# Pairwise products on two engines: fewer waits in VectorE's order, a larger VectorE share, one more cut in the first piece

## The chip, the cores and the metric

The kernel runs on one core of a Trainium2 chip. The metric is the device time of one execution in microseconds (us). Times before are of 14 executions; the profile is of one.

## The reference

The input is a matrix of 4096 rows and 256 columns in fp32. For each row, the output holds the product of every pair of its elements, upper triangle only, row by row of that triangle: 256 products with element 0, 255 with element 1, and so on, 32,896 in all.

```python
d = inputs.shape[1]
dot = jnp.einsum('bi,bj->bij', inputs, inputs)
iu, ju = jnp.triu_indices(d)
return dot[:, iu, ju]
```

The output has 539 MB and the input 4 MB.

## The kernel before

A partition holds 32 rows of the input, which are all loaded at the start (three loads, L246). The work goes by groups of two rows a partition (REPEAT = 2), 16 groups. The 32,896 columns of a group are cut into three pieces of 10,944, 10,976 and 10,976 columns (`even_borders`, L26). So there are 48 pieces; I call the three pieces of one group a row of pieces. A piece is computed into one of two places in on-chip memory (`places`, L123) and stored from there with one DMA of some 11 MB (L226). Of the first piece of all, four parts are stored on their own, cut at the columns in FIRST (L23), so that the stores can start early.

A piece consists of runs (`runs`, L31): the stretch of products of one element i with all j from i on. `split` (L71) gives the first runs of a piece to ScalarE and the rest to VectorE: it moves runs to ScalarE until VectorE's estimated time (`vector_time`, L67: 68 ns an operation and 1.046 ns an element) is within a budget of so many ns a column (BUDGETS, L22) or ScalarE would be the later one. ScalarE takes one activation for each run and group row (L206), with element i as its scale. VectorE takes one tensor_tensor for a run or for two runs together, both group rows at once (L185). An operation for two runs computes one junk element behind its second run, which the next operation of the same stretch overwrites. So the order on VectorE matters: `interleave` (L57) cuts VectorE's runs in two halves and takes operations from both in turn, and each operation waits until the operation two places before it has finished (`Work.add` with `back` 1, L144) and counts itself on the semaphore `v_own`.

Each engine runs its own loop over passes of six pieces (`all_pieces`, L230). Two pieces are made ahead of the loop. For each piece VectorE takes the place's semaphore `free` (L178; `take` at L134 waits and subtracts in one instruction), raises `go` for ScalarE (L179), computes, waits for its own last operation and raises `v_done` (L193). ScalarE takes `go` (L202), computes, waits for its last one and raises `a_done` (L215). SyncE takes both (L223, L224) and issues the store; the 16 DMA engines that carry it raise `free` by one each when their part has landed. At the start of a group VectorE and ScalarE copy its input rows into tiles of their own (L175, L199). The first piece's parts are counted on `head`, which GpSimd turns into `free` (L252).

Of the kernel before, what the change touches and what calls it, by code (L numbers as in the profile page):

```python
# [9 lines left out]
AF = mybir.ActivationFunctionType  # L10
ALU = mybir.AluOpType
# [3 lines left out]
REPEAT = 2  # L15
PIECES = 3
PLACES = 2
PASS = 6
AHEAD = 2


BUDGETS = [0.95, 0.8, 0.85]  # L22
FIRST = [512, 1536, 3584]  # L23


def even_borders(lo: int, hi: int, pieces: int) -> list[int]:  # L26
# [30 lines left out]
def interleave(block: list) -> list:  # L57


    half = len(block)  # L60
    while half and len(vector_ops(block[:half])) > len(vector_ops(block[half:])):
        half -= 1
    a, b = vector_ops(block[:half]), vector_ops(block[half:])
    return [op for k in range(max(len(a), len(b))) for ops in (a, b) for op in ops[k : k + 1]]


def vector_time(block: list) -> float:  # L67
# [15 lines left out]
def window(ap: bass.AP, free: list) -> bass.AP:  # L83
    return bass.AP(ap.tensor, ap.offset, [list(ap.ap[0]), *free])


@with_exitstack
def kernel(
    ctx: ExitStack, tc: tile.TileContext, x: bass.AP, out: bass.AP
):  # L90

    nc = tc.nc
    n, d = x.shape
    width = out.shape[1]
    each, groups = REPEAT * d, n // (P * REPEAT)
    rounds = PASS // PIECES
    passes = groups // rounds
    assert n % (P * REPEAT) == 0 and width == d * (d + 1) // 2 and width % UNIT == 0
    assert PASS % PLACES == 0 and AHEAD == PLACES and PASS % PIECES == groups % rounds == 0  # L110
    borders = even_borders(0, width, PIECES)
    spans = list(zip(borders, borders[1:]))
    slot = max(b - a for a, b in spans)

    x_in = x.rearrange("(p g) d -> p (g d)", p=P)
    x_out = out.rearrange("(p h q r) c -> h q p r c", p=P, q=rounds, r=REPEAT)

    pool = ctx.enter_context(tc.tile_pool(name="all", bufs=1))
    xt = pool.tile([P, passes, rounds * each], F32, name="x")

    xv = pool.tile([P, each + 1], F32, name="xv")
    xa = pool.tile([P, each], F32, name="xa")
    places = [pool.tile([P, REPEAT, slot], F32, name=f"o{k}") for k in range(PLACES)]  # L123
    ctx.enter_context(tc.tile_critical())  # L124

    def semaphore(name: str):
        return ctx.enter_context(nc.semaphore(name))

    free = [semaphore(f"free{k}") for k in range(PLACES)]
    head, v_done, a_done, go = (semaphore(s) for s in ("head", "v_done", "a_done", "go"))  # L130
    loads = [0, each, groups // 2 * each, groups * each]
    loaded = [semaphore(f"loaded{k}") for k in range(len(loads) - 1)]

    def take(engine, sem, value: int):  # L134
        engine.wait_ge(sem, value).then_inc(sem, -value)  # L135

    class Work:

        def __init__(self, engine, name: str):
            self.engine, self.sem, self.count, self.marked = engine, semaphore(name), 0, 0

        def add(self, ins, back: int, mark: bool = True):  # L144
            if self.count > back:
                ins._wait_ge(self.sem, self.count - back)
            if mark:
                ins.then_inc(self.sem, 1)
                self.count += 1

        def end(self):
            return self.engine.wait_ge(self.sem, self.count)

        def restart(self):
            self.engine.sem_inc(self.sem, -self.count)  # L155
            self.count = 0

    v, a = Work(nc.vector, "v_own"), Work(nc.scalar, "a_own")

    def x_of(h, q: int) -> bass.AP:  # L160
        return xt[:, bass.ds(h, 1), q * each : (q + 1) * each].rearrange("p o d -> p (o d)")

    def blocks(p: int, ahead: bool):

        lo, hi = spans[p % PIECES]
        cuts = [lo, *(FIRST if ahead and p == 0 else []), hi]
        for a, b in zip(cuts, cuts[1:]):
            block = runs(d, a, b)
            k = split(block, 0.0 if ahead else BUDGETS[p % PIECES] * REPEAT * (b - a))
            yield a - lo, b - lo, block[:k], block[k:], lo  # L170

    def vector(h, pieces: range, ahead: bool):
        for p in pieces:
            if p % PIECES == 0:
                v.add(nc.vector.tensor_copy(xv[:, :each], x_of(h, p // PIECES)), 0)  # L175
                v.end()
            if not ahead:
                take(nc.vector, free[p % PLACES], 16)  # L178
                nc.vector.sem_inc(go, 1)  # L179
            for _, _, _, block, lo in blocks(p, ahead):  # L180
                for (i, j, at, length), m in interleave(block):
                    at -= lo

                    v.add(
                        nc.vector.tensor_tensor(  # L185
                            places[p % PLACES][:, :, at : at + m * length],
                            window(xv[:, j:], [[d, REPEAT], [1, m], [1, length]]),
                            window(xv[:, i:], [[d, REPEAT], [1, m], [0, length]]),
                            ALU.mult,
                        ),  # L190
                        1,
                    )
                v.end().then_inc(v_done, 1)  # L193
        v.restart()

    def scalar(h, pieces: range, ahead: bool):
        for p in pieces:
            if p % PIECES == 0:
                a.add(nc.scalar.activation(xa, x_of(h, p // PIECES), AF.Copy), 0)  # L199
                a.end()  # L200
            if not ahead:
                take(nc.scalar, go, 1)  # L202
            for _, _, block, _, lo in blocks(p, ahead):
                todo = [(run, r) for run in block for r in range(REPEAT)]
                for (i, j, at, length), r in todo:
                    ins = nc.scalar.activation(  # L206
                        places[p % PLACES][:, r, at - lo : at - lo + length],
                        xa[:, r * d + j : r * d + j + length],
                        AF.Copy,
                        scale=xa[:, r * d + i : r * d + i + 1],  # L210
                    )
                if todo:
                    ins.then_inc(a.sem, 1)
                    a.count += 1
                a.end().then_inc(a_done, 1)  # L215
        a.restart()

    def sync(h, pieces: range, ahead: bool):
        for p in pieces:
            place = places[p % PLACES]  # L220
            parts = list(blocks(p, ahead))
            for lo, hi, *_, base in parts:
                take(nc.sync, v_done, 1)  # L223
                take(nc.sync, a_done, 1)  # L224
                to = x_out[bass.ds(h, 1), p // PIECES, :, :, base + lo : base + hi]
                nc.sync.dma_start(to.rearrange("o p r c -> p (o r) c"), place[:, :, lo:hi]).then_inc(  # L226
                    free[p % PLACES] if len(parts) == 1 else head, 16
                )

    def all_pieces(engine, pieces_of):  # L230
        pieces_of(0, range(AHEAD), True)
        if engine is not nc.sync:
            for sem in loaded[1:]:
                engine.wait_ge(sem, 16)
        kind = engine.engine
        with nc.Fori(
            0,
            passes,
            engines=OrderedEngineSet([kind]),
            head_slot={kind: 0} if engine is not nc.sync else {},  # L240
        ) as h:
            pieces_of(h, range(AHEAD, PASS), False)
            with engine.If(h < passes - 1):
                pieces_of(nc.s_assert_within(h + 1, 0, passes - 1), range(AHEAD), False)

    for (lo, hi), sem in zip(zip(loads, loads[1:]), loaded):  # L246
        nc.sync.dma_start(xt.rearrange("p h d -> p (h d)")[:, lo:hi], x_in[:, lo:hi]).then_inc(sem, 16)
    nc.vector.memset(xv[:, each:], 0.0)  # L248
    for engine in (nc.vector, nc.scalar):
        engine.wait_ge(loaded[0], 16)  # L250

    take(nc.gpsimd, head, 16 * (len(FIRST) + 1))  # L252
    nc.gpsimd.sem_inc(free[0], 16)
    for engine, pieces_of in ((nc.vector, vector), (nc.scalar, scalar), (nc.sync, sync)):
        all_pieces(engine, pieces_of)
    for k in range(PLACES):
        take(nc.sync, free[k], 16)
    for sem in loaded:
        take(nc.sync, sem, 16)

# [26 lines left out]
```

## Time and profile before

| | |
|---|---|
| median of 14 executions | 1273.59 us (1273.39 to 1273.87) |
| the profiled execution | 1273.57 us |
| its span in the profile | 1271.5 us |
| VectorE (DVE) busy | 915.4 us, 1712 instructions |
| ScalarE (ACT) busy | 606.4 us, 1837 instructions |
| DMA, mean over the span | 427 GB/s |
| a store of a whole piece, issue to landing | 33.1 us median |

The span runs from the first to the last instruction that the profile shows; 2.1 us of the execution's time lie around it. "DVEq", "ACTq" and "SPq" are the engines' sequencers, which wait, branch and issue. L135 is the body of the helper `take`, so a wait there is one for `free`, `go`, `v_done` or `a_done`, by engine. In the table by stage, the columns are: the stretch, its length, busy time and number of instructions of VectorE, ScalarE and GpSimd, the granted TensorE clock, the mean busy share of the 16 DMA engines, and what they moved in GB/s. A packet is put there in the stretch where it falls for the most part, so in stretches of one or two packets the share can go above one.

### The profile page before, as it was taken

Reading aid. Unit: us, or ns where it says so; the run is one execution under the profiler, and the core shown is the slowest. Engines: PE = TensorE matmul, PEld = TensorE weight load, DVE = VectorE, ACT = ScalarE, POOL = GpSimd, SP = SyncE. Lnnn points to the kernel's source line nnn. Section 1 sums busy time; section 2 is a strip of 40 time slices with the busy share of each in tenths; the row PEclk is TensorE's granted clock in tenths of the full one; section 3 lists DMA queues with packets and bytes.
Section 4 is the critical chain, followed back from the end, with each engine's and each line's share of the span. In section 5 each row is a group of like instructions: output and inputs, shape, how many; then the busy total and the mean of one; then the engine's idle time right before and its main releaser. Section 6 shows DMA issues by size and latency. Waiting matters only on the chain. (4 is left out here: it accounts for less than half of the span.)

```text
span 1271.5 us, 4308 instructions
## 1 busy us (share of the span) xinstructions
DVE 915.4 (72%) x1712; ACT 606.4 (48%) x1837; POOL 0.2 (0%) x4
## 2 busy tenths in 40 slices
DVE  8767786777768776687757877578776787677860
ACT  8625535354363533635337352473524635156350
POOL 0000000000000000000000000000000000000000
DMA  9999999999999999999999999999999999999998
GB/s 380 436 438 424 438 423 439 424 438 435 426 439 424 437 424 438 428 433 437 425 419 442 419 442 420 440 421 419 442 420 441 420 441 420 420 441 424 437 420 356
DMA packets 14310, 543.21 MB, mean 427 GB/s; under 512 B 864, under 2 KB 864, under 8 KB 1504
## 3 DMA queue, kind: packets, MB, share of 16 engines
q1 hardware_dynamic: 14304, 543.17, 99.3%
q14 instruction: 6, 0.05, 0.0%
HBM read 4.19 MB, written 538.97 MB: 427 GB/s over the span
## 5 line engine op out<-in xcount | busy, mean ns | idle before, releaser
L185 DVE TENSOR_TENSOR o<-xv 128x736 f32<-128x736 f32 (+61 forms) x1695 | 908.5, 616 | 311.6 <-DVEq L135 311.0
L206 ACT ACTIVATE o<-xa 128x198 f32<-128x198 f32 (+44 forms) x1820 | 595.1, 419 | 621.1 <-ACTq L135 620.6
L175 DVE COPY xv<-x 128x512 f32 (+1 forms) x16 | 6.8, 427 | 8.9 <-DVEq L155 4.2
L199 ACT ACTIVATE xa<-x 128x512 f32 (+1 forms) x16 | 10.1, 629 | 5.1 <-ACTq L155 3.4
L199 ACT ACT_TABLE_LOAD x1 | 1.3, 1283 | 3.9 <-DMA x<-in_r_inputs_dram 3.9
L248 DVE MEMSET xv<- 128x1 f32 x1 | 0.1, 59 | 1.0 <-SPq L124 1.0
L274 POOL MEMSET const-uint8-127<- 128x1 uint8 x1 | 0.1, 102 | 0.0
L274 POOL MEMSET const-bfloat16-1.0<- 128x1 bf16 x1 | 0.1, 101 | 0.0
L274 POOL MEMSET const-float32-0.0<- 128x1 f32 x1 | 0.1, 98 | 0.2 <-issue 0.2
L274 POOL MEMSET const-float32-1.0<- 128x1 f32 x1 | 0.1, 98 | 0.0
## 6 DMA issues: line engine op xcount, KB each, us to landing
out_dram<-o SPq DMA_DIRECT2D x32, 10976.0 KB, 33.1
out_dram<-o SPq DMA_DIRECT2D x15, 10944.0 KB, 30.7
out_dram<-o SPq DMA_DIRECT2D x1, 7360.0 KB, 20.0
x<-in_r_inputs_dram SPq DMA_DIRECT2D x1, 2048.0 KB, 13.1
out_dram<-o SPq DMA_DIRECT2D x1, 2048.0 KB, 12.6
x<-in_r_inputs_dram SPq DMA_DIRECT2D x1, 1792.0 KB, 7.3
out_dram<-o SPq DMA_DIRECT2D x1, 1024.0 KB, 11.0
out_dram<-o SPq DMA_DIRECT2D x1, 512.0 KB, 10.4
```

Of the source, the lines that this page charges most:

```text
L175: v.add(nc.vector.tensor_copy(xv[:, :each], x_of(h, p // PIECES)), 0)
L185: nc.vector.tensor_tensor(places[p % PLACES][:, :, at : at + m * length], window(xv[:, j:], [[d, REPEAT], [1, m], [1, length]]), window(xv ...
L199: a.add(nc.scalar.activation(xa, x_of(h, p // PIECES), AF.Copy), 0)
L206: ins = nc.scalar.activation(places[p % PLACES][:, r, at - lo : at - lo + length], xa[:, r * d + j : r * d + j + length], AF.Copy, scale=x ...
L248: nc.vector.memset(xv[:, each:], 0.0)
L274: nc = _bacc.Bacc("TRN2", target_bir_lowering=False, num_devices=1)
```

## The change

- BUDGETS goes from 0.95, 0.8, 0.85 to 1.0, 1.0, 0.95 ns a column and group row, so VectorE gets more runs of each piece and ScalarE fewer.
- FIRST gets a fourth cut at 6400: the first piece is stored in five parts.
- `interleave` cuts VectorE's runs in SETS stretches (2 in this version) with equal numbers of operations, and tells for each operation which earlier one of its stretch it has to follow: only one that comes behind an operation for two runs has such a predecessor.
- An operation waits only where it has such a predecessor that no earlier wait covers (for the predecessor or the operation two places before it, whichever is later), and only operations that are waited for count on `v_own`, besides the last of a piece where a wait for it follows.
- The place's `free` is no longer lowered at each piece: VectorE waits for 16, then 32, then takes 48, in the three uses of a place in a pass. Where it waits, that wait raises `go`; where it takes, an uncounted operation raises `go`. ScalarE's first activation waits for `go` itself, against a running count.
- At most pieces the last operation raises `v_done` or `a_done` itself; only at the last piece of a group (and of a range of pieces, on VectorE) does the engine still wait for its own last operation and then raise it.

```diff
+SETS = 2
-BUDGETS = [0.95, 0.8, 0.85]
-FIRST = [512, 1536, 3584]
+BUDGETS = [1.0, 1.0, 0.95]
+FIRST = [512, 1536, 3584, 6400]
...
 def interleave(block: list) -> list:
-    half = len(block)
-    while half and len(vector_ops(block[:half])) > len(vector_ops(block[half:])):
-        half -= 1
-    a, b = vector_ops(block[:half]), vector_ops(block[half:])
-    return [op for k in range(max(len(a), len(b))) for ops in (a, b) for op in ops[k : k + 1]]
+    sets, k = [], 0
+    for left in range(SETS, 0, -1):
+        share = -(-len(vector_ops(block[k:])) // left)
+        end = k
+        while end < len(block) and len(vector_ops(block[k : end + 1])) <= share:
+            end += 1
+        if left == 1:
+            end = len(block)
+        sets.append(vector_ops(block[k:end]))
+        k = end
+    order, last = [], {}
+    for step in range(max(map(len, sets))):
+        for s, ops in enumerate(sets):
+            if step < len(ops):
+                order.append((*ops[step], last.get(s)))
+                last[s] = len(order) - 1 if ops[step][1] == 2 else None
+    return order
...
     def vector(h, pieces: range, ahead: bool, done: int = 0) -> int:
...
             if not ahead:
-                take(nc.vector, free[p % PLACES], 16)
-                nc.vector.sem_inc(go, 1)
+                if use(p) < uses:
+                    nc.vector.wait_ge(free[p % PLACES], 16 * use(p)).then_inc(go, 1)
+                else:
+                    take(nc.vector, free[p % PLACES], 16 * uses)
             for _, _, _, block, lo in blocks(p, ahead):
-                for (i, j, at, length), m in interleave(block):
+                order = interleave(block)
+                own = (p + 1) % PIECES == 0 or p == pieces[-1]
+                counted, waits = {len(order) - 1} if own else set(), {}
+                for k, (*_, before) in enumerate(order):
+                    if before is not None and before > max(waits.values(), default=-1):
+                        waits[k] = max(before, k - 2)
+                        counted.add(waits[k])
+                lets_go = -1
+                if not ahead and use(p) == uses:
+                    lets_go = next(k for k in range(len(order)) if k not in counted)
+                number = {k: done + 1 + c for c, k in enumerate(sorted(counted))}
+                for k, ((i, j, at, length), m, _) in enumerate(order):
...
+                    if k in waits:
+                        ins._wait_ge(v_own, number[waits[k]])
+                    if k in counted:
+                        ins.then_inc(v_own, 1)
+                    if k == lets_go:
+                        ins.then_inc(go, 1)
+                done += len(counted)
-                v.end().then_inc(v_done, 1)
-        v.restart()
+                if own:
+                    nc.vector.wait_ge(v_own, done).then_inc(v_done, 1)
+                else:
+                    ins.then_inc(v_done, 1)
+        return done

     def scalar(h, pieces: range, ahead: bool):
...
-            if not ahead:
-                take(nc.scalar, go, 1)
...
+                if not ahead:
+                    turns += 1
+                    todo[0]._wait_ge(go, turns)
+                if not todo:
+                    nc.scalar.sem_inc(a_done, 1)
+                elif (p + 1) % PIECES:
+                    todo[-1].then_inc(a_done, 1)
+                else:
+                    todo[-1].then_inc(a_own, 1)
+                    done += 1
+                    nc.scalar.wait_ge(a_own, done).then_inc(a_done, 1)
...
     for k in range(PLACES):
-        take(nc.sync, free[k], 16)
+        take(nc.sync, free[k], 16 * uses)
```

More of the change, by code (lines that the diff above doesn't have):

```diff
@@ L135, in take @@
         engine.wait_ge(sem, value).then_inc(sem, -value)
[L137 to L158, printed above, removed]
+    v_own, a_own = semaphore("v_own"), semaphore("a_own")
     def x_of(h, q: int) -> bass.AP:
@@ L170, in blocks, with use, vector @@
             yield a - lo, b - lo, block[:k], block[k:], lo
-    def vector(h, pieces: range, ahead: bool):
+    uses = PASS // PLACES
+    def use(p: int) -> int:
+        return (p - AHEAD) % PASS // PLACES + 1
+    def vector(h, pieces: range, ahead: bool, done: int = 0) -> int:
         for p in pieces:
+            place = places[p % PLACES]
             if p % PIECES == 0:
-                v.add(nc.vector.tensor_copy(xv[:, :each], x_of(h, p // PIECES)), 0)
-                v.end()
+                ins = nc.vector.tensor_copy(xv[:, :each], x_of(h, p // PIECES))
+                if done:
+                    ins._wait_ge(v_own, done)
+                ins.then_inc(v_own, 1)
+                done += 1
+                nc.vector.wait_ge(v_own, done)
@@ L177, in vector @@
             if not ahead:
-                take(nc.vector, free[p % PLACES], 16)
-                nc.vector.sem_inc(go, 1)
+                if use(p) < uses:
+                    nc.vector.wait_ge(free[p % PLACES], 16 * use(p)).then_inc(go, 1)
+                else:
+                    take(nc.vector, free[p % PLACES], 16 * uses)
             for _, _, _, block, lo in blocks(p, ahead):
-                for (i, j, at, length), m in interleave(block):
-                    at -= lo
[L184 to L191, printed above, removed]
-                    )
@@ new lines, in vector @@
+                if not ahead and use(p) == uses:
+                    lets_go = next(k for k in range(len(order)) if k not in counted)
+                number = {k: done + 1 + c for c, k in enumerate(sorted(counted))}
+                for k, ((i, j, at, length), m, _) in enumerate(order):
+                    at -= lo
+                    ins = nc.vector.tensor_tensor(
+                        place[:, :, at : at + m * length],
+                        window(xv[:, j:], [[d, REPEAT], [1, m], [1, length]]),
+                        window(xv[:, i:], [[d, REPEAT], [1, m], [0, length]]),
+                        ALU.mult,
+                    )
+                    if k in waits:
+                        ins._wait_ge(v_own, number[waits[k]])
+                    if k in counted:
+                        ins.then_inc(v_own, 1)
+                    if k == lets_go:
+                        ins.then_inc(go, 1)
@@ L196, in scalar @@
+                done += len(counted)
[4 more added lines that the diff above has]
+        return done
     def scalar(h, pieces: range, ahead: bool):
+        done = turns = 0
         for p in pieces:
+            place = places[p % PLACES]
             if p % PIECES == 0:
-                a.add(nc.scalar.activation(xa, x_of(h, p // PIECES), AF.Copy), 0)
-                a.end()
@@ L201, in scalar @@
-            if not ahead:
-                take(nc.scalar, go, 1)
+                nc.scalar.activation(xa, x_of(h, p // PIECES), AF.Copy).then_inc(a_own, 1)
+                done += 1
+                nc.scalar.wait_ge(a_own, done)
             for _, _, block, _, lo in blocks(p, ahead):
[L204 to L207, printed above, removed]
+                todo = [
+                    nc.scalar.activation(
+                        place[:, r, at - lo : at - lo + length],
@@ L211, in scalar @@
                     )
[L212 to L216, printed above, removed]
+                    for i, j, at, length in block
+                    for r in range(REPEAT)
+                ]
+                if not ahead:
[7 more added lines that the diff above has]
+                    todo[-1].then_inc(a_own, 1)
+                    done += 1
+                    nc.scalar.wait_ge(a_own, done).then_inc(a_done, 1)
+        for sem, count in ((a_own, done), (go, turns)):
+            if count:
+                nc.scalar.sem_inc(sem, -count)
     def sync(h, pieces: range, ahead: bool):
@@ L230, in all_pieces @@
     def all_pieces(engine, pieces_of):
-        pieces_of(0, range(AHEAD), True)
+        done = pieces_of(0, range(AHEAD), True)
+        if engine is nc.vector:
+            nc.vector.sem_inc(v_own, -done)
         if engine is not nc.sync:
@@ L241, in all_pieces @@
         ) as h:
-            pieces_of(h, range(AHEAD, PASS), False)
+            done = pieces_of(h, range(AHEAD, PASS), False)
             with engine.If(h < passes - 1):
-                pieces_of(nc.s_assert_within(h + 1, 0, passes - 1), range(AHEAD), False)
+                nxt = nc.s_assert_within(h + 1, 0, passes - 1)
+                if engine is nc.vector:
+                    nc.vector.sem_inc(v_own, -vector(nxt, range(AHEAD), False, done))
+                else:
+                    pieces_of(nxt, range(AHEAD), False)
+        if engine is nc.vector:
+            nc.vector.sem_inc(v_own, -done)
     for (lo, hi), sem in zip(zip(loads, loads[1:]), loaded):
```

## The prediction, made before the changed kernel ran

> **What bounds the kernel now.** I began with the page's slices and its table of DMA queues:
>
> ```profile
> DMA  9999999999999999999999999999999999999998
> GB/s 380 436 438 424 438 423 439 424 438 435 426 439 424 437 424 438 428 433 437 425 419 442 419 442 420 440 421 419 442 420 441 420 441 420 420 441 424 437 420 356
> ...
> q1 hardware_dynamic: 14304, 543.17, 99.3%
> ```
>
> The 16 DMA engines are busy in every slice but the last, and the one queue fills 99.3% of their time with 543 MB. The stores set the end; the two compute engines only refill places between them. Next I took the waits and the groups, to see which engine waits for whom:
>
> ```profile
> L185 DVE TENSOR_TENSOR o<-xv 128x736 f32<-128x736 f32 (+61 forms) x1695 | 908.5, 616 | 311.6 <-DVEq L135 311.0
> L206 ACT ACTIVATE o<-xa 128x198 f32<-128x198 f32 (+44 forms) x1820 | 595.1, 419 | 621.1 <-ACTq L135 620.6
> ```
>
> VectorE (L185) stands idle for 311 us and ScalarE (L206) for 621 us, nearly all of it behind L135, the helper that takes a place's "free" or the "go". Compute is early, everywhere. Then the timeline of the last row of three pieces:
>
> ```profile
> 1165.94 20.75 DVE L185 TENSOR_TENSOR o<-xv 128x996 f32<-128x996 f32 x22 [6.82 <-DVEq L135]
> 1165.99 5.66 ACT L206 ACTIVATE o<-xa 128x256 f32<-128x256 f32 x14 [7.18 <-ACTq L135]
> 1187.06 50.57 SPq L226 DMA_DIRECT2D out_dram<-o  x3
> 1191.99 17.52 DVE L185 TENSOR_TENSOR o<-xv 128x768 f32<-128x768 f32 x24 [5.30 <-DVEq L135]
> 1192.02 12.49 ACT L206 ACTIVATE o<-xa 128x7 f32<-128x7 f32 x36 [20.37 <-ACTq L135]
> 1218.01 18.88 DVE L185 TENSOR_TENSOR o<-xv 128x468 f32<-128x468 f32 x60 [8.50 <-DVEq L135]
> 1218.04 18.39 ACT L206 ACTIVATE o<-xa 128x98 f32<-128x98 f32 x62 [13.52 <-ACTq L135]
> ```
>
> A fill takes 20.75, 17.52 or 18.88 us, and fills start 26 us apart, one store's length. Last, the table by stage, laid over the end of the last store:
>
> ```profile
> 1264.00:1266.00 2.00, 0.00 (x0) 0.00 (x0) 0.00 (x0) 1.00 0.82 351
> 1266.20:1267.80 1.60, 0.00 (x0) 0.00 (x0) 0.00 (x0) 1.00 0.06 27
> 1267.80:1269.40 1.60, 0.00 (x0) 0.00 (x0) 0.00 (x0) 1.00 0.06 27
> ```
>
> After 1266.1 us a DMA share of 0.06 is left, one engine in sixteen at 27 GB/s, until 1269.6 us. So one DMA engine, which I call the straggler, ends 3.6 us behind the other fifteen. The landing records of each store (sixteen increments) say how it came to that. The store that lands around 1187.86 has fifteen increments between 1187.77 and 1187.96 and the last at 1191.76; its lag is 1.8 us at the first whole piece, about 2 us at 300 us, and 3.4 to 4.0 us from 600 us on. The packets show the fifteen standing still for about 0.46 us, from 1187.5 to 1187.96, before the store issued at 1187.06 begins, while the straggler still works on the previous one. **The straggler is the bound**: it has no gap after 2 us, and the end is its work, not the fifteen engines' and not the fills.
>
> **What the Trainium skill says.** "DMA: Bandwidth & Descriptors", section "Specifications", gives the fabric's ceiling as 435 GB/s; the table by stage has 432, 432 and 431 GB/s over the three stores before 1217.4, so nothing is to be had from more overlap. The same page, "Why a DMA increments its semaphore by 16 and not by 1", says that only the full 16 means that all has landed; here a fill starts 0.26 us after the sixteenth increment (1165.68 to 1165.94), thus behind the straggler. The same page, "Latency and other measured facts", says that two of the sixteen engines are usually slower and calls its cause a guess; this trace has one, unnumbered. "VectorE: DVE Perf Modes", section "The DRAIN you can't avoid", reports that a semaphore after each of eight copies costs nothing over one after the last. The trace agrees as far as it goes: the 22 operations of the 20.75 us fill hold 18,384 elements a partition, and with 68 ns each (the planner's own figure) that leaves 1.047 ns an element, with no room for a stall by waits.
>
> **The change, part by part.**
>
> *Waits and counts.* The text has four stretches and every third, but SETS is 2, and the loop over `order` still finds nearly every operation two places behind its predecessor in the same stretch. Counting by the code: 104 to 108 counted operations in a row of three pieces against 106 before. So this edit is about nothing. The `free` and `go` traffic loses one or two sequencer steps a piece (0.02 us for L179 in the chain), on a path with slack: 0.
>
> *Larger share.* By the planner's budgets, elements and operations of VectorE go from 18,384/22 to 19,388/22 in the first piece of a row, 15,148/24 to 19,108/29 in the second, 13,922/60 to 15,622/63 in the third. At 1.047 ns and 68 ns: 21.8 us, 22.0 us, and 20.6 + 0.2 (what the third misses now, 18.88 against 18.66) = 20.9 us. ScalarE falls from 14, 36 and 62 operations to 10, 16 and 48, some 4, 5.5 and 15 us, always done before VectorE. The longest fill grows from 20.75 to 22.0 us. Does that reach the straggler? From its landing to the next store's first packet: 0.26 (start) + fill + 0.37 (1186.69 to 1187.06) + 0.9 (issue to first packet) = fill + 1.53. It has its other store to do meanwhile, and needs the new one 1191.41 - 1165.68 = 25.7 us after the landing (1191.41 is its landing at 1191.76 less the 0.35 us that lie between a last packet and its increment). So a fill may last 24.2 us; 22.0 leaves 2.2 us. What is late next is the fifteen: at the present lag they stand still whenever a fill exceeds 20.75 - 0.46 = 20.3 us, so now also in the second piece, by up to 1.7 us, until the lag settles lower, near 2.5 us. That costs nothing at the end. Cover gone means a fill over 24.2 us: then each excess counts once a piece.
>
> *What the straggler pays for the compute.* Its store takes 26.35 us beside the third piece's fill, 26.08 beside the first's, 26.01 (a smaller one) beside the second's, and 25.95 for the very last, with no compute beside it (25.88 for the smaller size, by bytes). The excess is 0.40, 0.13 and 0.14 us, 0.67 a row, about 10 us in all the 15.3 rows. The fifteen show none of it. It follows the number of instructions: 122, 36 and 60 products beside them, thus 3.3, 3.6 and 2.3 ns each; by VectorE's alone (60, 22, 24) 6.7, 5.9 and 5.8 ns. No view separates the two, so I bound it. If every instruction counts, sequencer steps too, a row goes from 252 to about 217: -14% of 0.67 is -0.09 us a row, -1.4 us. If only VectorE's count, 106 to 114 products give +8 x 6 ns = +0.05 a row, +0.7 us. If instructions and semaphore counts weigh alike (374 to 341), -9%, -0.9 us. I take this middle one.
>
> *One more border in the first piece.* It splits the 7360 KB store at 6400. The DMA engines are full from 2 us on anyway (the 4 MB input fills the hole), so an earlier store gains 0. It adds 16 packets to each engine: the measured packets (14336 B in 535 ns, 29440 B in 1091 ns) make a split one dearer by some 9 ns, x16 = +0.15 us. Bounds -0.1 to +0.3.
>
> *Sum.* The profiled execution took 1273.57 us (the median is 1273.59): 2.0 until the first packet, 1267.6 of the straggler, 1.9 to the end of the span at 1271.5, and 2.1 around it. 1273.57 - 0.9 + 0.15 = **1272.8 us**. Both bounds give 1272.2 to 1274.4 with the border's cost; another page of instructions fetched (309 ns a packet early in the trace) adds 0.3 either way.
>
> **Rivals.** *ScalarE's instructions are what slows the straggler.* For it: its packets beside ScalarE's work are longer than those beside VectorE alone (1635 against 1630 ns in the first piece's fill). Against it: by ScalarE's counts the excess is 6.5, 9.3 and 3.9 ns, a worse fit. 112 to 74 takes a third, 0.23 us a row, 3.5 us: 1270.2 us. *Nothing that matters changes*, or VectorE's operations alone matter: counts stay, the bound stays, 1273.8 to 1274.4, say 1274.1 us. *Slower: the fill becomes the bound.* If the k - 2 waits held VectorE after all, by 60 ns an operation, the third piece would take 20.9 + 3.8 = 24.7 us, over the 24.2 by 0.5, less the 0.2 that the next store gives back: 15 times 0.3 us, 1278 us. It decides from 24.2 us on. Against it: the same waits stand in the kernel before, and the idle time on VectorE is all behind L135.
>
> **How the numbers follow.** A measurement of this kernel tells about 0.2% from no change, 2.5 us: the border lies at 1271.0 and 1276.1. Likeliest, as summed, 0.56 (1271.6 to 1273.6); VectorE alone or nothing, 0.25; ScalarE's relief, 0.14, nearly all of it beyond 0.2%; fill-bound, 0.05. So faster 0.13, same 0.82, slower 0.05. The range takes in the first two and the better half of the relief: 1270.5 to 1274.6.
>
> **What would show it.** Fills of about 21.8, 22.0 and 20.9 us on VectorE and still 16 DMA engines in lockstep; a tail of one engine of about 2.5 instead of 3.6 us; rows of 78.35 us instead of 78.45 between the straggler's landings. It is wrong if rows are shorter than 78.25 (ScalarE's relief) or a fill exceeds 24 us and the straggler shows a gap before a store. A change in the first 70 us of more than 0.5 us would mean that I misread the border.

## The result and the profile after

The changed kernel takes 1291.13 us (1290.98 to 1291.20) against 1273.58 us: the ratio is 1.0138, with a 95% interval of 1.0128 to 1.0148. It is 17.5 us slower, where 1272.8 us was forecast. The kernel before was timed again beside each experiment, at a median of 1273.49 to 1273.64 us; ratios and differences below are to that time.

The page of the changed kernel, its slices and its DMA queue:

```profile
DMA  9999999999999999999999999899998999999999
GB/s 381 444 421 430 436 393 414 436 434 416 413 414 436 434 428 401 414 436 435 435 393 414 436 435 435 371 436 435 435 435 386 421 435 436 414 413 414 435 436 392
...
q1 hardware_dynamic: 14576, 543.17, 98.0%
```

The bytes of the stores are the same, but the engines' share has fallen from 99.3 to 98.0%, and slices of 371 to 414 GB/s stand between slices at 435. The stores now have holes. The groups of the page tell that VectorE isn't what fills the time (columns: busy time and mean of one; then the idle time before them and what ended most of it):

```profile
L202 DVE TENSOR_TENSOR o<-xv 128x124 f32<-128x124 f32 (+61 forms) x1818 | 1023.2, 643 | 217.1 <-DMA out_dram<-o 148.0
L231 ACT ACTIVATE o<-xa 128x253 f32<-128x253 f32 (+38 forms) x1236 | 401.7, 416 | 826.5 <-DVEq L183 446.3
```

VectorE still idles for 217 us. ScalarE idles for 826 us, and only 446 of them end with `go` where VectorE waits (L183). The table of waits shows the rest (total, times, longest):

```profile
ACT o L231 <- DVEq L183: 446.3, 26, 22.0
ACT o L231 <- DVE o L202: 379.6, 14, 32.2
DVE o L202 <- DMA out_dram<-o: 148.0, 31, 6.3
```

The second line is new. Fourteen times ScalarE is released by one of VectorE's own products, after as long as 32 us. The timeline of one pass shows where:

```profile
1102.51 21.80 DVE L202 TENSOR_TENSOR o<-xv 128x1004 f32<-128x1004 f32 x22 [4.60 <-DVEq L148]
1123.86 4.08 ACT L231 ACTIVATE o<-xa 128x256 f32<-128x256 f32 x10 [32.16 <-DVE o L202]
1128.19 49.12 SPq L263 DMA_DIRECT2D out_dram<-o  x3
1128.57 21.99 DVE L202 TENSOR_TENSOR o<-xv 128x808 f32<-128x808 f32 x29 [4.26 <-DVEq L148]
1150.04 19.95 ACT L231 ACTIVATE o<-xa 128x7 f32<-128x7 f32 x64 [22.10 <-DVE o L202]
```

VectorE works on a piece from 1102.51 to 1124.31 us. ScalarE's ten products for the same piece start at 1123.86, and the store is issued at 1128.19, behind ScalarE. The next piece has the same form: VectorE is at work from 1128.57 and ScalarE starts at 1150.04 (the 64 include the next piece's 48). In the kernel before, both engines start a piece within 0.05 us of each other. In these two pieces of six the two engines work in turn.

The code says why. In a place's third use VectorE waits for `free` and lowers it in the same instruction, and the raising of `go` is left to the first operation that counts on nothing else (`lets_go`). With two stretches nearly every operation is counted: in the pieces concerned the first uncounted one is number 21 of 22 and number 27 of 29.

### The profile page after: what moved, and what is told of

Same layout as the page of the kernel before. It is cut to its first block, busy times and chain, and to the rows that moved or that the text cites. A ratio compares the mean times of both kernels' runs of the same rounds, so it can differ in the third digit from the quotient of the medians.

```text
span 1289.0 us, 3720 instructions
## 1 busy us (share of the span) xinstructions
DVE 1030.0 (80%) x1835; ACT 413.1 (32%) x1253; POOL 0.2 (0%) x4
## 5 line engine op out<-in xcount | busy, mean ns | idle before, releaser
L202 DVE TENSOR_TENSOR o<-xv 128x124 f32<-128x124 f32 (+61 forms) x1818 | 1023.2, 643 | 217.1 <-DMA out_dram<-o 148.0
L231 ACT ACTIVATE o<-xa 128x253 f32<-128x253 f32 (+38 forms) x1236 | 401.7, 416 | 826.5 <-DVEq L183 446.3
## 6 DMA issues: line engine op xcount, KB each, us to landing
out_dram<-o SPq DMA_DIRECT2D x1, 2816.0 KB, 15.3
```

The lines of the kernel that those rows point to most:

```text
L202: ins = nc.vector.tensor_tensor(place[:, :, at : at + m * length], window(xv[:, j:], [[d, REPEAT], [1, m], [1, length]]), window(xv[:, i:] ...
L231: nc.scalar.activation(place[:, r, at - lo : at - lo + length], xa[:, r * d + j : r * d + j + length], AF.Copy, scale=xa[:, r * d + i : r ...
```

## The experiments

The theory, **late go**: in the third use of each place, ScalarE's time is added to VectorE's, the two fills become 25.4 us (21.35 until ScalarE starts, and 4.08) and 27.0 us (21.47 and 5.49), over the 24.2 us that the prediction worked out as the limit. The rival: the **larger share** as such, fills of 22 us, is too much for the stores.

**go raised before the first operation** (the rest of the change stays):

```diff
                     take(nc.vector, free[p % PLACES], 16 * uses)
+                    nc.vector.sem_inc(go, 1)
...
-                if not ahead and use(p) == uses:
+                if False:
                     lets_go = next(k for k in range(len(order)) if k not in counted)
```

> The changed kernel, but in a place's third use VectorE raises go before its first operation, as the kernel before does at every piece, and not from an uncounted operation near the end. Theory L (late go: in two of six pieces of a pass ScalarE starts when VectorE is nearly done, and the store waits for both in turn): the stalls of 1.7 us at these pieces go, and the time is 1273 to 1274.5 us, about that of the kernel before. Rival S (the larger share itself: fills of 22 us come too late for the stores): fills of VectorE stay at 21.8, 22.0 and 20.9 us, so the time stays at 1289 to 1292 us. Rival N (the fewer instructions, waits and borders matter by some other way): in between.

Measured: 1271.86 us (ratio to before 0.9986, interval 0.9979 to 0.9992). All of the loss is gone, and 1.8 us more, so the time lies below the 1273 to 1274.5 us that the late go alone had. Its timeline, the same two pieces:

```profile
1086.00 4.08 ACT L232 ACTIVATE o<-xa 128x256 f32<-128x256 f32 x10 [10.82 <-DVEq L186]
1086.06 21.79 DVE L203 TENSOR_TENSOR o<-xv 128x1004 f32<-128x1004 f32 x22 [4.66 <-DVEq L148]
1112.08 5.49 ACT L232 ACTIVATE o<-xa 128x7 f32<-128x7 f32 x16 [21.99 <-DVEq L186]
1112.13 21.98 DVE L203 TENSOR_TENSOR o<-xv 128x808 f32<-128x808 f32 x29 [4.28 <-DVEq L148]
```

VectorE's fills are as long as in the changed kernel, 21.79 and 21.98 us, and start 26 us apart: the larger share isn't the cause.

**Four stretches in place of two:**

```diff
-SETS = 2
+SETS = 4
```

> The changed kernel with SETS = 4 in place of 2. By the code a third of the operations are then counted (36 to 37 in a row of three pieces in place of 108) and the first operation of a piece is an uncounted one, so that go is raised at its end, some 1.2 us into the piece. Theory L: 1272.5 to 1274.5 us, like a_go_first. Rival S: 1289 to 1292 us. Side question, what slows the one late DMA engine: if semaphore counts do, its excess of 0.67 us a row falls by some 0.4 and the time by 5 to 6 us more, to 1267 to 1269 us; if instructions do, there is nothing beyond a_go_first.

Measured: 1270.75 us (0.9977, 0.9968 to 0.9986). One number undoes the loss, since the first operation of a piece is now free to raise `go`, and ScalarE starts 1.2 us into the piece:

```profile
1085.02 21.86 DVE L202 TENSOR_TENSOR o<-xv 128x1004 f32<-128x1004 f32 x23 [4.62 <-DVEq L148]
1086.26 4.08 ACT L231 ACTIVATE o<-xa 128x256 f32<-128x256 f32 x10 [11.98 <-DVE o L202]
```

The time is 1.1 us below the kernel with `go` first. The two 95% intervals overlap, but the executions of the two kernels don't (1270.58 to 1270.94 against 1271.65 to 1272.06 us). The gain is far below the 5 to 6 us that counts alone would have given, and not the nothing of the instructions.

**The old share in the changed kernel:**

```diff
-BUDGETS = [1.0, 1.0, 0.95]
+BUDGETS = [0.95, 0.8, 0.85]
```

> The changed kernel with the budgets of the kernel before (0.95, 0.8, 0.85): VectorE's fills are 20.75, 17.5 and 18.9 us again, ScalarE has 14, 36 and 62 operations (5.7, 12.5 and 19 us). Theory L: go still comes with the end of VectorE's work in two pieces of six, and there ScalarE's work is added to it: 20.75 - 0.5 + 5.7 = 26.0 and 17.5 - 0.5 + 12.5 = 29.5 us against 25.4 and 27.0 in the changed kernel. The two stalls of a pass grow from 3.4 to about 5.7 us, seven passes have them: 1291 + 16 = 1307 us (1302 to 1312). Rival S: the share is undone, so 1272 to 1275 us.

Measured: 1308.77 us (1.0276, 1.026 to 1.0292). The rival would have had this kernel the fast one; the late go had 1307. Its timeline shows what is added:

```profile
1143.71 17.51 DVE L202 TENSOR_TENSOR o<-xv 128x768 f32<-128x768 f32 x24 [5.34 <-DVEq L148]
1143.77 48.34 SPq L263 DMA_DIRECT2D out_dram<-o  x3
1160.66 30.77 ACT L231 ACTIVATE o<-xa 128x7 f32<-128x7 f32 x98 [17.15 <-DVE o L202]
```

ScalarE's 36 products (of the 98) begin at 1160.66, when VectorE's 17.51 us are nearly over. So the larger share of VectorE doesn't cause the loss but softens it.

**The larger share alone, in the kernel before:**

```diff
-BUDGETS = [0.95, 0.8, 0.85]
+BUDGETS = [1.0, 1.0, 0.95]
```

> The kernel before with the new budgets alone (1.0, 1.0, 0.95). Theory L: go comes first as ever, the longest fill is 22.0 us and below the 24.2 that the late DMA engine leaves: 1272.5 to 1274.5 us. Rival S: the fills of 22 us are the cause: 1286 to 1292 us. If ScalarE's operations are what slows the late DMA engine, 112 to 74 a row make it 1270 us; if VectorE's operations do (106 to 114), 1274 us.

Measured: 1272.58 us (0.9992, 0.9983 to 1.0). Fills of 22 us cost nothing, and both engines start them together:

```profile
1112.66 21.98 DVE L185 TENSOR_TENSOR o<-xv 128x808 f32<-128x808 f32 x29 [4.29 <-DVEq L135]
1112.69 5.49 ACT L206 ACTIVATE o<-xa 128x7 f32<-128x7 f32 x16 [21.98 <-ACTq L135]
```

**The late go alone, in the kernel before:**

```diff
                 take(nc.vector, free[p % PLACES], 16)
-                nc.vector.sem_inc(go, 1)
+                if p >= AHEAD:
+                    nc.vector.sem_inc(go, 1)
...
                 v.end().then_inc(v_done, 1)
+            if not ahead and p < AHEAD:
+                nc.vector.sem_inc(go, 1)
```

> The kernel before with one thing of the change put in: in the two pieces of a pass that use a place for the third time, go is raised after VectorE's last operation and not before its first. Theory L: these two fills become 20.75 + 0.1 + 5.7 = 26.5 and 17.5 + 0.1 + 12.5 = 30.1 us, with some 1.5 us around them against 26 us of a store; two stalls of 2.7 and 3.6 us, seven times, less what the late DMA engine no longer adds: 1312 us (1307 to 1316). If the late go costs only together with the other edits: below 1290 us.

Measured: 1316.06 us (1.0334, 1.0318 to 1.035), just above the 1307 to 1316 us expected. The timeline shows that the hand-over took 0.3 us and not the 0.1 of the estimate:

```profile
1123.62 20.75 DVE L186 TENSOR_TENSOR o<-xv 128x996 f32<-128x996 f32 x22 [6.41 <-DVEq L135]
1144.67 5.65 ACT L209 ACTIVATE o<-xa 128x256 f32<-128x256 f32 x14 [27.84 <-ACTq L135]
...
1150.62 49.02 SPq L229 DMA_DIRECT2D out_dram<-o  x3
```

VectorE ends at 1144.37, ScalarE starts at 1144.67. The late go needs no other part of the change.

**go raised half way** (in the changed kernel):

```diff
-                    lets_go = next(k for k in range(len(order)) if k not in counted)
+                    lets_go = len(order) // 2
...
                     if k == lets_go:
-                        ins.then_inc(go, 1)
+                        nc.vector.wait_ge(v_own, number[k - 2])
+                        nc.vector.sem_inc(go, 1)
```

> The changed kernel with go raised half way through VectorE's operations in a place's third use (behind a wait for the operation two places before the middle one) in place of near the end. ScalarE then starts some 11 us into the piece and needs 4.1 or 5.5 us, so it is done at 15 or 17 us, before VectorE's 21.8 or 22.0. Theory L: a late go costs nothing until ScalarE would end after VectorE, so 1271.5 to 1272.5 us, like a_go_first. If every microsecond of delay costs: half of the 19 us, 1281 us.

Measured: 1271.87 us (0.9986, 0.9979 to 0.9993), within 0.01 us of the kernel with `go` first:

```profile
1112.15 21.98 DVE L202 TENSOR_TENSOR o<-xv 128x808 f32<-128x808 f32 x29 [4.29 <-DVEq L148]
1123.20 5.52 ACT L232 ACTIVATE o<-xa 128x7 f32<-128x7 f32 x16 [22.31 <-DVEq L214]
```

ScalarE starts 11 us late, ends at 1128.7, and VectorE at 1134.1. Eleven of the 21 us of delay are free, as the shorter engine has that slack.

**The fourth cut alone**, in the kernel before (`FIRST = [512, 1536, 3584, 6400]`).

> The kernel before with the fourth cut of the first piece alone. Each DMA engine gets 16 packets more, estimated at +0.15 us from the packet times; the engines are full from 2 us on, so nothing is won at the start: 1273.5 to 1274.0 us. A rival: the cut lets pieces be freed or instructions be fetched in another order in the first 70 us, which would show as -0.5 to -1 us, as much as b_share gained beyond its rows.

Measured: 1273.48 us (0.9999, 0.999 to 1.0007): no effect that could be told.

**What the late DMA engine pays for.** Three kernels leave products out of the loop of the kernel before (the first leaves out ScalarE's, the second VectorE's, the third both, but two a piece and engine), by these lines; where VectorE's go, a piece of a place that nothing else would write is set to zero at the start:

```diff
+                if not ahead:
+                    todo = todo[:2]
...
-                for (i, j, at, length), m in interleave(block):
+                for (i, j, at, length), m in interleave(block)[-2:] if not ahead else interleave(block):
```

> The kernel before without all but two of ScalarE's products of a piece in the loop, so that its output is incomplete: it leaves that part of the computation out, to see what the late DMA engine pays for ScalarE's instructions. If VectorE's operations alone slow it: 1273 to 1274 us. If all instructions do (112 of some 252 a row go): the excess falls from 0.67 to about 0.38 us a row, 1269 us.

> The kernel before without all but two of VectorE's products of a piece in the loop; this part of the computation is left out, to see what the late DMA engine pays for VectorE's instructions. If VectorE's operations slow it: its excess of 0.67 us a row all but goes, the other fifteen engines with their 78.05 us a row decide, 1265 to 1267.5 us. If all instructions do: 0.40 us a row are left, 1269.5 us.

> The kernel before with both engines' products in the loop left out, but two of a piece and engine: the stores alone, the floor for any division of the work. Every theory of the late engine: 1264 to 1267 us; if it stays above 1270 us, compute is not what slows that engine at all.

Measured: 1269.73 us (0.9969, 0.9957 to 0.9981) without ScalarE's, 1268.05 us (0.9957, 0.9942 to 0.9972) without VectorE's, 1265.99 us (0.994, 0.9925 to 0.9956) without both. The page of the last one:

```profile
DVE 72.2 (6%) x155; ACT 71.1 (6%) x187; POOL 0.2 (0%) x4
...
q1 hardware_dynamic: 14304, 543.17, 99.9%
```

With next to no compute the same stores fill 99.9% of the engines' time, and the kernel is 7.5 us faster. So compute costs the stores 7.5 us in the kernel before, and it does so through the late engine (the straggler of the prediction). Its landings give the length of a row (the mean of five rows late in each run); its lag is its last landing less the median of the other fifteen:

| kernel | a row at the last landing, us | its lag at the end, us | time, us |
|---|---|---|---|
| before | 78.50 | 3.8 | 1273.58 |
| before, larger share | 78.44 | 2.4 | 1272.58 |
| changed, go first | 78.41 | 2.5 | 1271.86 |
| changed, four stretches | 78.33 | 2.4 | 1270.75 |
| without ScalarE's products | 78.25 | 3.5 | 1269.73 |
| without VectorE's products | 78.15 | 2.4 | 1268.05 |
| without both | 77.99 | 0.5 | 1265.99 |

Taking 106 products of ScalarE's out of a row saves 0.25 us, 2.4 ns each; 100 of VectorE's, 0.35 us, 3.5 ns each. That VectorE's operations alone matter (1273 to 1274 us without ScalarE's) is ruled out. That all instructions weigh alike had 1269 and 1269.5 us for the first two kernels; the second measured 1.5 us less, though its interval (1266.1 to 1269.9 us) still reaches that.

These prices are rough. The two savings make 0.60 us, and leaving out both saves 0.51: there all sixteen engines land within 0.7 us of each other, and the other fifteen, whose rows take 78.0 us in all three of these kernels, can set the pace. Counted up from that kernel, ScalarE's products cost 0.16 us a row (1.5 ns each) and VectorE's 0.26 us (2.6 ns each). Nor is it shown that the number of products is what counts. By busy time, 35 us of ScalarE's work a row and 55 us of VectorE's were left out, which makes 7.2 and 6.4 ns per us, nearly alike. The excess store by store in the prediction (0.40, 0.13 and 0.14 us beside 37, 26 and 30 us of busy time) follows the products better, but no run separates the two.

**Eight stretches:** (`SETS = 8`)

> The changed kernel with SETS = 8: every seventh operation waits and counts (some 15 counts a row in place of 36 with SETS = 4 and 108 with 2), go is raised with the first operation of a piece. If counts cost the late DMA engine about 1 us per 70 in a row, as a_sets4 against a_go_first has it (1.1 us), another 21 fewer give 0.3 us: 1270.4 us (1270.2 to 1270.6). If the gain of a_sets4 came from something that is there once only: 1270.75 us or more.

Measured: 1270.33 us (0.9975, 0.9965 to 0.9985), within what the price by counts had, though the code has 18 or 19 counts a row and not 15. It has the lowest time of the complete kernels, 3.2 us ahead of the kernel before; its lead over four stretches (0.0002 in the ratio) is not resolved, and its late rows take 78.32 us against 78.33.

## Why the prediction was wrong, point by point

**What bounds the kernel before: right.** With next to no compute the stores take 1266 us, and the rest is the late engine's.

**The step that failed is "Waits and counts".** It says: "So this edit is about nothing. The `free` and `go` traffic loses one or two sequencer steps a piece [...] on a path with slack: 0." It had found 104 to 108 counted operations in a row (the code gives 108 or 109), and stopped there. The same count says that hardly an operation is free to raise `go`, so that in a place's third use `go` moves from before VectorE's first operation to its 21st or 27th. I read what the edit removes (a step) and not where the raising of `go` was moved to and who is behind it: ScalarE. From this the next step took a false sentence, ScalarE's work "always done before VectorE", which holds in four pieces of six.

With that step mended, its own limit gives the result, with the fills as measured afterwards. They are 25.4 and 27.0 us against 24.2: 1.2 us for the first, 27.0 - 24.2 - 1.2 = 1.6 for the second, since the first stall gives the second that much room. That is 2.8 us a pass and 20 us in seven passes. Measured against the kernel with `go` first, the landings fall behind by 3.8 us in the first pass and by 2.5 or 2.6 in each of the other six, 19.1 us in all. In these six the two stores concerned land 27.1 and 27.8 us after the one before, instead of 26.0 and 26.3: stalls of 1.1 and 1.5 us. With `go` first, or half way, they are gone.

**The larger share: right.** Fills of 21.8, 22.0 and 20.9 us were forecast, 21.80, 21.99 and 20.89 us measured. That they don't reach the stores is shown by the share alone (1272.58 us). That the lag would settle near 2.5 us is seen there (2.4) and with `go` first (2.5). In the changed kernel itself it isn't: each pair of stalls lets the late engine catch up, and its lag ends at 0.6 us.

**The late engine's price: about the size, not the form.** Forecast was -0.9 us for the whole change. The share alone gave -1.06 us: 38 products of ScalarE fewer at 2.4 ns and 8 of VectorE more at 3.5 make -0.06 us a row, over 15.3 rows -1.0; within the interval of that run, 0 to -2.2 us, this can't be more than a fit. The whole change with `go` first gave -1.8 us. The 0.7 us between them aren't resolved; fewer waiting and raising instructions fit, but no run takes these away alone.

**The border: nothing,** as forecast (+0.15, measured -0.15, within an interval of about 1 us to either side).

**The rivals.** Slower by the fill becoming the bound had 0.05, with VectorE held by its waits as the mechanism. The bound became the fill indeed, with 24.2 us as the point from which it decides, but by ScalarE being held and not VectorE. Its sign for this, a fill over 24 us, came true once a fill is taken to the end of the later engine. That the change doesn't do what its words say was seen (two stretches, not four) and priced at nothing; it was the whole of the loss.

## What to carry to other kernels

When a semaphore is raised from another place than before, find the instruction that now raises it and its number in the queue, and follow who waits for it; that it is still raised once a piece says nothing on when. Two engines that share a piece must start together, or the later one must have the slack: here a delay of 11 us was free and one of 21 us cost 1.4%. A choice by "the first that is free" depends on other numbers, here on SETS, and turns bad without a word when these change.

## What the runs showed of the hardware that I had not expected

One DMA engine of sixteen is slowed while the compute engines work, and the fifteen others hardly: its row takes 78.50 us in the kernel before, 78.25 without ScalarE's products and 78.15 without VectorE's, while theirs take 78.0 in the kernels with one or neither. Divided by products, that is 1.5 to 2.4 ns for each of ScalarE's, which count on a semaphore once a piece, and 2.6 to 3.5 ns for each of VectorE's, which count one by one; these are estimates from the four rows. Counting less seems to give back part of it: with four stretches (37 or 38 counts a row in place of 108 or 109) a row is 0.08 us shorter, some 1.1 ns for each count saved, and the kernel 1.1 us faster. What the engine has to do with the compute, and whether the recording of the profile has a part in it, no run here tells; the times are of executions like the one profiled.

VectorE itself gains little from fewer waits: the third piece's fill takes 20.78 us with 64 operations in four stretches and 20.88 us with 63 in two.
